# Two chained cross-attentions on one core: the last four heads' image outputs moved to GpSimd, the image softmax's shift moved within its step, and unread products in eleven steps

## The chip, the core and the metric

The kernel runs on one core of a Trainium2 chip. The metric is device time in microseconds (us) of one execution. Five engines work side by side, each through its own instructions in order: PE multiplies matrices (its weight loads are listed apart, as PEld), DVE (VectorE), ACT (ScalarE) and POOL (GpSimd) work element by element, and SP here only issues transfers (DMAs). [...]

## The reference

The input is x, 64 batches of 256 tokens with 320 channels, and a context of 77 rows of 512 per batch, of which the last four are image rows. Two layers follow each other; both have 20 heads of 16 channels and end with a projection, a bias and the residual. Layer 0 attends to the context. Layer 1 is this, for one batch:

```python
text_ehs, ip_ehs = encoder[:, :-4], encoder[:, -4:]
probs_t = softmax(q @ k_t * scale)               # 73 text rows
text_out = probs_t @ v_t
qsem = l2norm(probs_t @ text_ehs)
sem = qsem @ l2norm(ip_ehs)                       # 4 image rows
probs_ip = softmax(q @ k_ip * scale + 0.5 * sem) * spatial_mask
ip_out = probs_ip @ v_ip
out = (text_out + ip_out) @ W_out + b_out + residual
```

(The program's layer 0 takes all 77 rows in one softmax as its text, since layer 0's text length is 77 and leaves no image rows.) All of it is computed in float32.

## The kernel before

**Pairs, units, steps.** The batches go in 32 pairs p. A pair holds 1024 channel-major values of x per channel block: two blocks of 128 channels ("main") and a third of 64 for each batch, both batches stacked on 128 partitions ("last"). A unit is one batch, 128 tokens and eight heads; `UNITS` lists five of them per batch, the fifth being the last four heads (16 to 19) of both token halves. So a pair has ten units, and the main loop over g has ten steps for each pair. In the text, p and k are g divided by ten, and the remainder; a turn is the ten steps of one p. Step g works on layer 0's unit g and on layer 1's unit g - 13 (`LAG`), so layer 1 of a pair is one to two turns behind layer 0.

**One step.** In PSUM a single tile sc (L1082, one buffer) takes three results in turn: `semantics` (L755 and L761: layer 1's exponentials of the step before against the Gram matrix of the context, the values and ones), then `scores` (L641) of both layers. DVE takes each layer's row maximum (mx, L659) and subtracts it (w, L661); ACT exponentiates (L669, L672 and L673); for layer 0 DVE sums (L687, L688) and GpSimd normalizes (`normalize`, L692). PE transposes the exponentials of the unit before (L705, L706; layer 1's first, then layer 0's), ACT copies them out (L712, L713, L731, L732), and `attend` (L788, L793) multiplies layer 0's by the values. DVE multiplies the semantics by the weights (prod, L772 and L775) and ACT copies the text sums out of sc (sums, L1064); only then may the next step's L755 write sc. Each step ends with L1136.

**Fillers.** `fillers(k, p)` lists other work by step in three lists that the loop puts at three places: projections of queries, keys, values and outputs (L334, L379, L528 to L570, L616), the Gram matrix (`gram`, L493: PE, then two ACT copies, three small GpSimd operations and nine DMAs), the masked keys (`keys_by_head`, L365, GpSimd), the placing of values and Gram matrix into the matrices gv and gr that `semantics` multiplies by (`place_values`, L424 to L444, and `place_gram`, L511 and L515, GpSimd). A helper, `keep_order` (L46), ties the instructions of PE, ACT, DVE and GpSimd to the order in which the loop writes them; only SP's order of transfers is left to the scheduler after the first turn. The last steps, which have few fillers, hold unread transposes of the identity (`keep_busy`, L741).

**Layer 1's image part.** When the fifth unit of a batch has its semantics (k=9 for the pair's first batch, k=4 for the second), GpSimd squares the text's sums (least, L866), DVE completes the norms (L870, L882), `text_output` (an, L821 and L850) divides the text outputs by their sums, token by token. One step later `image_scores` (L883, L884) forms the four image scores of each head (num), two steps later `image_shifted` (L889 on DVE, L890 on GpSimd) subtracts their maximum and `image_exponential` (L893, ACT) follows, at the start of the step; three steps later `image_weights` (L900 to L902, L850) normalizes them into iw. `text_transposed` (L837, L838) turns an into aT at k=0 and k=5, in three transposes for each 128 tokens: two for main and one for last. At k=7 PE transposes the weights of all 20 heads (`image_transposed`, L914). The image values are in DRAM rows (vip_rows): for each batch, twenty DMAs (L475) put copies of its four rows under each other, and a GpSimd multiplication by ip_mask (L480) keeps of copy h the channels of head h only. `image_attend` (L926) multiplies these for main at k=8, ACT copies the result (L936) and GpSimd adds it to main (L938); `image_attend_last` (L947) does it for last, in two matmuls over 80 rows, and DVE adds (L951). Then `project` (L528, L537) runs at k=9 and `project_last` (L616) at the next k=0.

Of the kernel before, what the change touches and what calls it, by code (L numbers as in the profile page):

```python
# [14 lines left out]
H = 20  # L15
D = 16
# [47 lines left out]
def tile_two_cross_attentions(ctx: ExitStack, tc: tile.TileContext, a: dict, out: bass.AP):  # L64
# [179 lines left out]
    head_mask = blocks("head_mask", P, 8, D)  # L244
    for n in (4, 2):
        nc.gpsimd.tensor_add(head_mask[:, :n], head_mask[:, :n], head_mask[:, n : 2 * n])
    ip_mask = blocks("ip_mask", H * NIP, H, NIP)

# [218 lines left out]

    def image_values(p, b):  # L470

        n, r0 = H * NIP, (2 * p + b) * NIP
        vip = vips[p, b] = big.tile([n, C], F32, tag="vip", name=f"vip{p}_{b}", bufs=3)
        for h in range(H):
            nc.sync.dma_start(vip[h * NIP : (h + 1) * NIP, :], vip_rows[r0 : r0 + NIP, :])  # L475

    def place_image_values(p, b):
        n, vip = H * NIP, vips[p, b]
        v = vip.rearrange("p (h d) -> p h d", d=D)
        nc.gpsimd.tensor_tensor(v, v, ip_mask[:n].unsqueeze(2).broadcast_to([n, H, D]), ALU.mult)  # L480

    grams = {}

# [247 lines left out]
        nc.scalar.copy(pt[:, :, s * P : (s + 1) * P], ps)  # L731
        nc.scalar.copy(rt[:, s * P : (s + 1) * P], pr[:n, 0, :])  # L732

    def keep_busy(n):


        if n:
            ps = ptr.tile([P, 4, P], F32, tag="tr", name=f"busy{len(busy)}")
            busy.append(n)
            for i in range(n):  # L740
                nc.tensor.transpose(ps[:, i % 4, :], ident, ident)  # L741
# [72 lines left out]
            nc.scalar.copy(last, ps[:, 1, :])  # L814


    def text_output(p, b):

        sums = stats[p, b][1]
        rec = small.tile([P, 2 * H], F32, tag="rec", name=f"rec{p}_{b}", bufs=2)  # L820
        nc.vector.reciprocal(rec, sums[:, :, NIP + D])  # L821
        an = big.tile([P, 2, H, D], F32, tag="an", name=f"an{p}_{b}", bufs=1)
        by_head(an, sums[:, :, NIP : NIP + D], rec)
        return an

    def text_transposed(p, b):

        an = made["an"]
        if b == 0:
            aTs[1, p] = channels("aT1", f"aT1_{p}", 1)  # L830
        main, last = aTs[1, p]
        rows = slice(b * HALF, (b + 1) * HALF)
        for s in range(2):
            ps = ptr.tile([P, 4, P], F32, tag="tr", name=f"atr{p}_{b}{s}")
            t = an[:, s].rearrange("p h d -> p (h d)")
            for i in range(2):
                nc.tensor.transpose(ps[:, i, :], t[:, i * P : (i + 1) * P], ident)  # L837
            nc.tensor.transpose(ps[: rows.stop, 2, :], t[:, C - rows.stop :], ident)  # L838
            t0 = b * S + s * P
            nc.scalar.copy(main[:, :, t0 : t0 + P], ps[:, :2])  # L840
            nc.scalar.copy(last[rows, s * P : (s + 1) * P], ps[rows, 2, :])

    one = const.tile([P, 1], F32, tag="one", name="one")

    def by_head(to, t, factor):

        n = t.shape[2]
        for s, h0, at in ((0, 0, 0), (1, HT, H), (1, 0, H + 4)):
            m = H if s == 0 else H - HT if h0 else HT
            nc.gpsimd.tensor_tensor(  # L850
                to[:, s, h0 : h0 + m], t[:, at : at + m],
                factor[:, at : at + m].unsqueeze(2).broadcast_to([P, m, n]), ALU.mult,
            )


    nums = {}
# [38 lines left out]
    def image_weights(p, b):  # L895

        num = nums[p, b]
        m = small.tile([P, 2, H], F32, tag="imx", name=f"imx{p}_{b}", bufs=1)
        r = m.rearrange("p s h -> p (s h)")
        nc.vector.tensor_reduce(r, num, AX.X, ALU.add)  # L900
        nc.vector.reciprocal(r, r)
        nc.gpsimd.tensor_mul(m, m, smask.unsqueeze(2).broadcast_to([P, 2, H]))  # L902
        to = weights[p, b] = small.tile([P, 2, H, NIP], F32, tag="iw", name=f"iw{p}_{b}", bufs=2)
        by_head(to, num, r)

    weights = {}

    def image_transposed(p):
        n = H * NIP
        ps = ptr.tile([P, 4, P], F32, tag="tr", name=f"itr{p}")  # L910
        for b in range(2):
            w = weights[p, b].rearrange("p s h t -> p s (h t)")
            for s in range(2):
                nc.tensor.transpose(ps[:n, 2 * b + s, :], w[:, s], ident)  # L914
        wT = big.tile([n, S2], F32, tag="iwT", name=f"iwT{p}", bufs=1)
        nc.scalar.copy(wT, ps[:n].rearrange("p j t -> p (j t)"))
        return wT
# [22 lines left out]
        t = big.tile([P, 2, S2], F32, tag="ip_out", name=f"ip_out{p}", bufs=1)  # L940
        return [lambda i=i: out_of(i) for i in range(2)]

    def image_attend_last(p):
        wT, last = made["wT"], aTs[1, p][1]
        ps = pms.tile([P, 512], F32, tag="ms", name=f"ipv{p}_2")
        for b in range(2):
            nc.tensor.matmul(  # L947
                ps[b * HALF : (b + 1) * HALF, :S], vips[p, b][:, 2 * P :], wT[:, b * S : (b + 1) * S],
                start=True, stop=True,
            )  # L950
        nc.vector.tensor_add(last, ps[:, :S], last)  # L951


    made = {}

    def fillers(k, p):
# [19 lines left out]
        elif k == 1:  # L976
# [3 lines left out]
                add(1, p, place_values, 0, p, 0)  # L980
            add(0, p, queries, 0, p, 2)
            add(1, p - 1, project, 0, p - 1)
            add(1, p - 1, place_gram, 0)
            add(1, p, keys_by_head, 0, p, 1)
            add(1, p - 1, keys_by_head, 1, p - 1, 0)
# [9 lines left out]
        elif k == 3:  # L995
            add(0, p + 1, load_context, p + 1)
            add(0, p - 1, queries, 1, p - 1, 2)
            if p == 0:
                add(1, p, image_keys, 0)
            add(1, p - 1, queries, 1, p - 1, 1)  # L1000
            add(1, p, place_values, 0, p, 1)
            add(1, p - 1, keys_by_head, 1, p - 1, 1)
        elif k == 4:
            if p == 0:
                add(0, p, image_keys, 1)
            else:
                add(0, p, keys, 1, p, 0)
            add(1, p - 1, values, 1, p - 1, 1)
            add(1, p + 1, first_queries, p + 1)
        elif k == 5:  # L1010
            if p == 0:
                add(0, p, image_keys, 2)
            add(0, p + 1, keys, 0, p + 1, 0)
            add(2, p - 2, text_transposed, p - 2, 1)
        elif k == 6:
            while len(made_rows) * P < min(NB, 2 * (p + 2)) * T:
                rows_todo.extend((len(made_rows), l) for l in range(2))
                made_rows.append(rows_todo[-1])
            for n in range(len(rows_todo) // 2):
                add(0, p, value_rows, *rows_todo.pop(0))  # L1020
            if p == 0:
                add(0, p, image_norms)
            else:
                add(1, p, keys, 1, p, 1)
            add(1, p - 1, gram, p - 1, 1)
            add(1, p, place_image_keys, p)
        elif k == 7:
            add(0, p + 1, keys, 0, p + 1, 1)
            add(1, p + 1, last_keys, p + 1)
            add(1, p - 2, lambda: made.update(wT=image_transposed(p - 2)))  # L1030
            add(1, p - 1, place_values, 1, p - 1, 1)
            add(1, p - 1, image_values, p - 1, 0)
            if p == 0:
                add(1, p, image_rows)
        elif k == 8:
            while rows_todo:
                add(0, p, value_rows, *rows_todo.pop(0))
            add(1, p - 1, place_gram, 1)
            add(1, p + 1, keys_by_head, 0, p + 1, 0)
            add(1, p - 1, image_values, p - 1, 1)  # L1040
            add(1, p - 2, image_attend_last, p - 2)
            add(3, p - 2, lambda: held.update(i=lambda: image_attend(p - 2)))
        else:
            add(0, p - 2, project, 1, p - 2)
            add(1, p + 1, values, 0, p + 1, 0)
            for b in range(2):
                add(1, p - 1, place_image_values, p - 1, b)
# [18 lines left out]
            image_least(*before1[:2])  # L1066

    last0 = last1 = before1 = None
    later, early = {}, {}
    for g in range(NP * NU + LAG + 12):  # L1070
        p, k = divmod(g, NU)
        first, second, third, begin = fillers(k, p)
# [25 lines left out]
        for l in range(2):  # L1098
            if now[l]:
                shifted(ps, l, *now[l])  # L1100
        new1 = None
        if last1:
            transposed(1, *last1)
# [23 lines left out]
            sums_out(ps)  # L1127
        if now[1]:
            exponential(1, g, *now[1])
        for fn, args in later.pop(g, ()):  # L1130
            fn(*args)
        if now[0]:
            normalize(g)
        if before1:
            q, b, u = before1[:3]
            nc.vector.tensor_reduce(eight(stats[q, b][2], u), prod, AX.X, ALU.add)  # L1136
            if ends:
                image_squares(q, b)
                made["an"] = text_output(q, b)
                later[g + 1] = [(image_scores, (q, b))]  # L1140
                early[g + 2] = [(image_shifted, (q, b)), (image_exponential, (q, b))]
                early[g + 3] = [(image_weights, (q, b))]
        for fn, args in second:
            fn(*args)
# [3 lines left out]
                attend(q, b, int(u > 1))  # L1148
        for fn, args in third:
            fn(*args)  # L1150
        if ends:
            image_norm(*before1[:2])
        last0 = (*now[0], ws[0]) if now[0] else None
# [53 lines left out]
```

## Time and profile before

| | us |
|---|---|
| median of 3 runs | 2615.54 (2613.35 to 2617.14) |
| the profiled execution | 2612.19 |
| its span, first to last instruction | 2610.4 |
| busy: PE | 2552.0 (98%) |
| busy: DVE | 1971.3 (76%) |
| busy: ACT | 1535.6 (59%) |
| busy: POOL | 1439.9 (55%) |
| DMA packets of the main queue | 153432, 18.0% of 16 engines |
| granted PE clock, mean | 0.998 |

A row of the profile reads: start or line, engine, operation, the written tile and the read ones (`out<-in`), shapes as partitions x elements, and how many. In brackets stands the idle time before it and what ended it. A matmul's own duration is longer than its share of PE's time, since the next one starts before it ends; for PE it is the distance of starts that counts.

### The profile page before, as it was taken

The page shows a single profiled execution, that of the slowest core. Times are in us where ns is not written, and L with a number is a line of the kernel's source. Part 1 is how long each engine was busy: PE and PEld are TensorE (multiplying, and loading weights), DVE is VectorE, ACT ScalarE, POOL GpSimd, SP SyncE. Part 2 cuts the span into 40 slices and gives each one's busy share as a digit, 9 for nine tenths or more (in the row PEclk, how much of TensorE's full clock was granted, in tenths as well). Part 3 has the DMA queues.
Part 4 walks back from the last instruction along what each step waited for, and adds up shares of the span by engine and source line. Part 5 has one row for each costly group of instructions (what it writes and reads, how often), then busy time and mean ns, then how long its engine had stood idle before and what let it go on. Part 6 is the DMA issues. An engine that isn't in the chain of part 4 may idle for free.

```text
span 2610.4 us, 74097 instructions
## 1 busy us (share of the span) xinstructions
PE 2552.0 (98%) x27026; PEld 1979.1 (76%) x27026; DVE 1971.3 (76%) x3641; ACT 1535.6 (59%) x3989; POOL 1439.9 (55%) x3514
## 2 busy tenths in 40 slices
PE   7999999999999999999999999999999999999998
PEld 5677777777777777777777777777777777777677
DVE  4577777777787777787777787777777778777864
ACT  3465665665665665665665665665665566666553
POOL 2456555566555556555556555556555565555542
PEclk9999999999999999999999999999999999999999
DMA  5212211112111112111112111112111112111100
GB/s 164 72 29 58 58 43 48 43 51 55 52 51 38 51 51 55 55 48 39 51 52 55 51 52 43 47 52 56 52 51 39 51 53 55 47 50 34 29 22 23
DMA packets 154658, 132.28 MB, mean 51 GB/s; under 512 B 48248, under 2 KB 132984, under 8 KB 154296
## 3 DMA queue, kind: packets, MB, share of 16 engines
q1 hardware_dynamic: 153432, 126.38, 18.0%
q8 instruction: 217, 3.56, 0.6%
q14 instruction: 145, 1.19, 0.2%
q10 hardware_dynamic: 864, 1.15, 0.1%
HBM read 89.53 MB, written 33.91 MB: 47 GB/s over the span
## 4 chain that ended last, share of the span: by engine, by line
PE 84%; DVE 7%; DMA 3%; ACT 2%; POOL 1%; issue 1%; SPq 1%; DVEq 0%; POOLq 0%; ACTq 0%
PE sc L755 12%; PE tr L705 11%; PE o_ps L528 8%; PE sc L641 7%; PE v_ps L379 6%; PE sc L761 4%; PE q_ps L528 4%; PE q_ps L555 4%; PE k_ps L334 3%; PE o_ps L616 3%; DVE w L661 3%; PE pv L788 2%; PE o_ps L537 2%; DVE mx L659 2%; PE q_ps L557 2%; PE rtr L706 2%
## 5 line engine op out<-in xcount | busy, mean ns | idle before, releaser
L659 DVE TENSOR_REDUCE mx<-sc 128x8 f32<-128x584 f32 (+1 forms) x640 | 497.3, 777 | 446.9 <-PE sc L641 446.8
L692 POOL TENSOR_TENSOR parts<-w,sm 128x512 f32<-128x512 f32 (+1 forms) x640 | 439.5, 707 | 301.9 <-ACT parts L673 177.8
L661 DVE TENSOR_TENSOR w<-sc,mx 128x616 f32<-128x616 f32 x640 | 511.8, 800 | 67.0 <-ACT w L669 0.5
L712 ACT COPY pt<-tr 128x512 f32<-128x512 f32 x320 | 186.8, 584 | 431.9 <-PE tr L705 427.5
L705 PE MATMUL tr<-ident,parts 128*128 128x128 f32 x2560 | 409.6, 283 | 12.5 <-POOL parts L692 5.2
L755 PEld LDWEIGHTS sc<-gv,pt 64*128 64x128 f32 x5120 | 316.9, 187 | 96.0 <-ACT sums L1064 47.3
L705 PEld LDWEIGHTS tr<-ident,parts 128*128 128x128 f32 x2560 | 282.5, 141 | 123.4 <-issue 88.0
L755 PE MATMUL sc<-gv,pt 64*128 64x94 f32 x5120 | 356.3, 278 | 17.4 <-ACT sums L1064 17.2
L676 POOL COPY att<-w 128x32 f32<-128x32 f32 x320 | 66.8, 209 | 469.7 <-DVE w L661 469.2
L669 ACT ACTIVATE w<-w 128x616 f32<-128x616 f32 x320 | 232.0, 725 | 96.7 <-DVE w L661 95.8
L687 DVE TENSOR_REDUCE sm<-w 128x8 f32<-128x616 f32 x320 | 247.9, 775 | 13.6 <-ACT w L669 13.6
L641 PE MATMUL sc<-kbd,q 32*128 32x154 f32 x5120 | 248.2, 306 | 1.0 <-ACT q L586 0.8
L528 PE MATMUL o_ps<-aT,wo 128*128 128x256 f32 x1024 | 231.6, 379 | 0.0
L1136 DVE TENSOR_REDUCE nrm<-prod 128x8 f32<-128x584 f32 x320 | 227.3, 710 | 0.4
L772 DVE TENSOR_TENSOR prod<-sc,parts 128x512 f32<-128x512 f32 x320 | 217.8, 681 | 4.0 <-PE sc L761 4.0
L528 PEld LDWEIGHTS o_ps<-aT,wo 128*128 128x128 f32 x1024 | 189.7, 190 | 23.0
L672 ACT ACTIVATE parts<-w 128x512 f32<-128x512 f32 x320 | 207.1, 647 | 0.0
L641 PEld LDWEIGHTS sc<-kbd,q 32*128 32x128 f32 x5120 | 187.0, 187 | 6.2 <-issue 5.4
L731 ACT COPY pt<-tr 128x512 f32<-128x512 f32 x256 | 151.1, 590 | 67.1 <-PE tr L705 66.8
L379 PE MATMUL v_ps<-wv,cf 128*128 128x320 f32 (+1 forms) x624 | 182.1, 438 | 0.0
L706 PE MATMUL rtr<-ident,parts 128*104 128x128 f32 (+1 forms) x640 | 174.8, 273 | 0.0
L1064 ACT COPY sums<-sc 128x168 f32<-128x168 f32 x320 | 96.4, 301 | 122.5 <-DVE prod L775 121.3
(151 smaller groups left out, 4840.0 us busy)
## 6 DMA issues: line engine op xcount, KB each, us to landing
vip<-vip_rows SPq DMA_DIRECT2D x1280, 5.0 KB
out_dram<-x SPq DMA_DIRECT2D x64, 256.0 KB
x<-in_x_dram SPq DMA_DIRECT2D x31, 512.0 KB
v_rows<-vs SPq DMA_DIRECT2D x38, 320.0 KB
vm<-v_rows SPq DMA_DIRECT2D x152, 80.0 KB
ct<-in_ctx_dram SPq DMA_DIRECT2D x32, 308.0 KB
cf<-in_ctx_dram SPq DMA_DIRECT2D x38, 256.0 KB
g_rest<-gram_rest SPq DMA_DIRECT2D x512, 0.5 KB
```

The costliest lines, as they stand in the source:

```text
L379: nc.tensor.matmul(ps[:n, :C], cfs[i][:, k, :n], wv[l][:, k, :], start=(k == 0), stop=(k == KE - 1))
L528: nc.tensor.matmul(ps[b][:, m, :], w[:, k, m * P : (m + 1) * P], main[:, k, b * S : (b + 1) * S], start=(k == 0 and m == 0), stop=False,)
L641: nc.tensor.matmul(ps[:, r, 2 * T * l : 2 * T * (l + 1)], q[rows, b, :] if part == 2 else q[rows, t0 : t0 + P], kbd[rows, part].rearrange( ...
L659: nc.vector.tensor_reduce(mx, sc[:, :, :, :nt], AX.X, ALU.max)
L661: nc.vector.tensor_tensor(w, sc, mx.unsqueeze(3).broadcast_to([P, 4, 2, T]), ALU.subtract)
L669: nc.scalar.activation(w, w, AF.Exp, scale=SCALE)
L687: nc.vector.tensor_reduce(sm, w, AX.X, ALU.add)
L692: nc.gpsimd.tensor_tensor(two[:, 8 * t0 : 8 * t1].rearrange("p (h t) -> p h t", h=8), w[:, :, t0:t1], sm.unsqueeze(2).broadcast_to([P, 8, ...
L705: nc.tensor.transpose(ps[:, i, :], flat[:, i * P : (i + 1) * P], ident)
L706: nc.tensor.transpose(pr[:n, 0, :], flat[:, 4 * P : 4 * P + n], ident)
L755: nc.tensor.matmul(ps[:, i % 2 * 2 + j, at : at + GV], pt[half_rows, i, :], gv[b][half_rows, part, i, :], start=start and i < 2, stop=False,)
L1136: nc.vector.tensor_reduce(eight(stats[q, b][2], u), prod, AX.X, ALU.add)
```

## The change

Four things change.

1. The last four heads' image outputs. Each batch's image values are loaded for 16 heads (sixteen DMAs of 256 channels), the weights are transposed for 16 heads, and `image_attend_last` is gone. In its place a DMA spreads the batch's four rows of the last 64 channels over all 128 partitions (vlast, one buffer), and GpSimd multiplies them, token by token, by the weights of the last four heads and adds the products to the text output (four times a multiplication and an addition, each 128 wide). The last heads' text outputs of both batches go into one tile (an_last); `text_transposed` transposes main alone, and two transposes and one copy (`last_transposed`, at k=8) bring an_last into last. `last_image_outputs` runs at k=4 for the first batch and at k=7 for the second.
2. The shift. `image_shifted` stands behind both layers' subtractions, before layer 1's transposes, in place of the start of the step; `image_exponential` goes into the list `later`, and that list is put behind `normalize` in place of before it. So `image_scores` stands behind `normalize` too.
3. Two fillers move: the second batch's `gram` from k=6 to k=5, and its `place_values` from k=7 to the end of GpSimd's work of k=8.
4. `keep_busy` can use the PSUM pool of the fillers (ms), and eight unread transposes are put at the end of the steps g = 6, 7, 9, 10, 18, 19 and of 314 to 318 (p=31, k=4 to 8).

```diff
     def image_values(p, b):
-        n, r0 = H * NIP, (2 * p + b) * NIP
-        vip = vips[p, b] = big.tile([n, C], F32, tag="vip", name=f"vip{p}_{b}", bufs=3)
-        for h in range(H):
-            nc.sync.dma_start(vip[h * NIP : (h + 1) * NIP, :], vip_rows[r0 : r0 + NIP, :])
+        n, r0 = HT * NIP, (2 * p + b) * NIP
+        vip = vips[p, b] = big.tile([n, 2 * P], F32, tag="vip", name=f"vip{p}_{b}", bufs=3)
+        for h in range(HT):
+            nc.sync.dma_start(vip[h * NIP : (h + 1) * NIP, :], vip_rows[r0 : r0 + NIP, : 2 * P])
...
+    def last_image_values(p, b):
+        r0 = (2 * p + b) * NIP
+        v = vips[p, b, "last"] = small.tile([P, NIP, HALF], F32, tag="vlast", name=f"vlast{p}_{b}", bufs=1)
+        nc.sync.dma_start(v, vip_rows[r0 : r0 + NIP, 2 * P :].unsqueeze(0).broadcast_to([P, NIP, HALF]))
...
-            nc.tensor.transpose(ps[: rows.stop, 2, :], t[:, C - rows.stop :], ident)
             t0 = b * S + s * P
             nc.scalar.copy(main[:, :, t0 : t0 + P], ps[:, :2])
-            nc.scalar.copy(last[rows, s * P : (s + 1) * P], ps[rows, 2, :])
+    def last_image_outputs(p, b):
+        v = vips[p, b, "last"].rearrange("p t (h d) -> p t h d", d=D)
+        w, to = weights[p, b, "last"], lasts[p][:, :, b]
+        part = [P, 2, H - HT, D]
+        for t in range(NIP):
+            prod = small.tile(part, F32, tag="ip_last", name=f"ip_last{p}_{b}{t}", bufs=1)
+            nc.gpsimd.tensor_tensor(
+                prod, v[:, t].unsqueeze(1).broadcast_to(part), w[:, :, :, t].unsqueeze(3).broadcast_to(part), ALU.mult
+            )
+            nc.gpsimd.tensor_add(to, to, prod)
+    def last_transposed(p):
+        ps = pms.tile([P, 512], F32, tag="ms", name=f"ltr{p}")
+        for s in range(2):
+            nc.tensor.transpose(
+                ps[:, s * P : (s + 1) * P], lasts[p][:, s].rearrange("p b h d -> p (b h d)"), ident
+            )
+        nc.scalar.copy(aTs[1, p][1], ps[:, :S])
...
-    def image_attend_last(p):
-        wT, last = made["wT"], aTs[1, p][1]
-        ps = pms.tile([P, 512], F32, tag="ms", name=f"ipv{p}_2")
-        for b in range(2):
-            nc.tensor.matmul(
-                ps[b * HALF : (b + 1) * HALF, :S], vips[p, b][:, 2 * P :], wT[:, b * S : (b + 1) * S],
-                start=True, stop=True,
-            )
-        nc.vector.tensor_add(last, ps[:, :S], last)
...
+            add(1, p - 2, last_image_values, p - 2, 0)
...
+            add(1, p - 2, last_image_outputs, p - 2, 0)
...
+            add(1, p - 1, gram, p - 1, 1)
             add(2, p - 2, text_transposed, p - 2, 1)
+            add(1, p - 2, last_image_values, p - 2, 1)
...
-            add(1, p - 1, gram, p - 1, 1)
...
-            add(1, p - 1, place_values, 1, p - 1, 1)
+            add(1, p - 2, last_image_outputs, p - 2, 1)
...
-            add(1, p - 2, image_attend_last, p - 2)
+            add(1, p - 1, place_values, 1, p - 1, 1)
+            add(1, p - 2, last_transposed, p - 2)
...
+        if g in middle:
+            fn, args = middle.pop(g)
+            fn(*args)
         new1 = None
         if last1:
             transposed(1, *last1)
...
+        if now[0]:
+            normalize(g)
         for fn, args in later.pop(g, ()):
             fn(*args)
-        if now[0]:
-            normalize(g)
...
-                early[g + 2] = [(image_shifted, (q, b)), (image_exponential, (q, b))]
+                middle[g + 2] = (image_shifted, (q, b))
+                later[g + 2] = [(image_exponential, (q, b))]
                 early[g + 3] = [(image_weights, (q, b))]
...
+        if g in (6, 7, 9, 10, 18, 19) or -6 <= idle <= -2:
+            keep_busy(8, pms, "ms")
```

## The prediction

> **What bounds the kernel now.** I read the busy times on the profile's page first, then the waits, then the timeline of one steady turn (the ten steps of one p; here p=15, from 1167 us on), then the last 30 us.
>
> ```profile
> span 2610.4 us, 74097 instructions
> ...
> PE 2552.0 (98%) x27026; PEld 1979.1 (76%) x27026; DVE 1971.3 (76%) x3641; ACT 1535.6 (59%) x3989; POOL 1439.9 (55%) x3514
> ...
> PE 84%; DVE 7%; DMA 3%; ACT 2%; POOL 1%; issue 1%; SPq 1%; DVEq 0%; POOLq 0%; ACTq 0%
> ```
>
> PE is nearly always busy and carries the chain, so what counts is PE's own work per step, until a step gets so short that the next shortest chain ends it. A step begins at its first L755 row. Read off these rows, the median steps k=0 to 9 last 8.08, 9.39, 8.61, 7.45, 8.69, 6.42, 6.95, 6.96, 7.09 and 7.81 us, and hardly vary from turn to turn. The boundary k=5 to k=6, PE's rows:
>
> ```profile
> 1215.26 0.38 PE L837 MATMUL atr<-ident,an 128*128 128x128 f32 x2
> 1215.47 0.27 PE L838 MATMUL atr<-ident,an 128*128 128x128 f32 x1
> 1216.07 1.13 PE L755 MATMUL sc<-gv,pt 64*128 64x94 f32 x16 [0.32 <-ACT sums L1064]
> ```
>
> Here PE is out of work: only one buffer holds sc, and L755 may not write it before DVE has done mx, w, mx, w, prod and ACT the copy sums. That chain (mx starts 2.06 to 2.16 us into a step, sums ends 6.36 to 6.54) is the floor of a step: 6.42 in k=5, 6.59 in steps 314 and 318. Nine of ten steps stand above it and are PE's.
>
> **The edits, step by step.** (Pitch means from one start to the next; a transpose's is 0.11 us, as in L837's two rows.)
>
> *k=0 and k=5, text_transposed.* Each loses two third transposes (L838): 0.22 us. In k=0 that is gained. In k=5 the moved gram comes in: its eight L493 rows hold PE from 1222.39 to 1223.02, 0.63 us, and cost 0.53 here, since what follows L706 then starts 0.11 after it instead of 0.20. PE's work was 6.42 - 0.39 = 6.03 and becomes 6.03 - 0.22 + 0.53 = 6.34, under the floor: k=5 stays at 6.42, and gram is free there.
>
> *k=6.* Without gram PE has 6.95 - 0.63 and, for the changed neighbour of L755, + 0.08 = 6.40. But the shift's DVE reduction L889 (309 ns) now stands between the second w and prod. Followers start about 0.08 before the end of the one ahead, so it adds 0.23 to the floor: sums ends at 6.44 in this step (1222.51), L755 follows 0.05 after it, 6.44 + 0.05 + 0.23 = 6.72. Gain 0.23. In the six turns with two value rows in k=6 (9.10 us) PE still binds and the gain is 0.55.
>
> *k=8.*
>
> ```profile
> 1236.28 0.27 PE L706 MATMUL rtr<-ident,parts 128*104 128x128 f32 x1
> 1236.37 0.30 ACT L1064 COPY sums<-sc 128x168 f32<-128x168 f32 x1
> 1236.48 0.20 PEld L947 LDWEIGHTS ipv<-iwT,vip 80*64 80x64 f32 x4 [0.18 <-issue]
> 1236.49 0.65 PE L947 MATMUL ipv<-iwT,vip 80*64 80x256 f32 x4
> ```
>
> From L706 to the next L755 (1237.07) are 0.79 us. Two transposes in L947's place make 0.11 + 0.11 + 0.20 = 0.42. Sums ends at 6.69 in this step, so the floor is 6.74: 7.09 becomes 6.74, a gain of 0.35. The new transposes wait for GpSimd's second sums, ready at 5.65 by the paragraph after the next; PE comes to them at 6.39, so 0.7 covers them, and behind them only L755 waits. The transposes of the weights lose columns (80 to 64) and nothing in time: L706's 104 and 128 columns both pass in 0.11.
>
> *k=1.* ACT's exponential L893 stood ahead of the copies pt and pr and waited for GpSimd until 3.35 us into the step; the second transposes, which need those copies' PSUM buffers, began at 4.31. In k=3, the same work without it, they begin at 4.17. L893 goes behind the exponentials: 0.14 gained. Its reader in k=2 (L900) sits in DVE's wait for PE.
>
> *GpSimd.* The other splits come out even: an's three products took 744 + 295 + 631 and become 631 + 400 + 631, the mask L480 shrinks from 728 to about 630. Per pair 16 operations of 128 wide are new. Multiplications: 295 ns at 64 and 631 at 256 (L850); L464, 128 wide, took 400, which I take. Additions: 523 at 160 (L884), so 0.45. Each waits for the one before, and L883 to L884 shows 0.07 between such. Eight take 4 x 0.85 + 7 x 0.07 = 3.9 us (bounds 2.8, all at the 64-wide row, and 5.5, all at the 256-wide one). The first eight run in k=4 and 5, where GpSimd was idle from 1211.3 to 1215.0. The second eight take the place of place_values, which goes from k=7 to behind the masked keys in k=8, into this gap:
>
> ```profile
> 1240.85 0.44 POOL L365 TENSOR_TENSOR kbd<-kl,head_mask 128x154 f32<-128x154 f32 x1
> 1244.82 0.27 POOL L866 TENSOR_TENSOR least<-sums 128x40 f32<-128x40 f32 x1 [3.52 <-ACT sums L1064]
> ```
>
> From k=8's start: normalization ends at 1.73, the eight at 5.65; then by their rows' pitches L938 2.31, att 0.17, L692 1.32, L511 0.92, L515 0.27, L365 1.06, place_values 3.48: 15.2. Steps 8 and 9 now last 14.55, so it ends 0.6 into k=0. Its last product is read by L761, 1.06 into k=0: 0.4 us to spare. Behind it least comes 0.65 later, and DVE's L870 and the four x of k=0 with it; g_ps needs the third x, at 1.83 + 0.65 = 2.48, and starts at 2.62: covered.
>
> *SP and DMA.* Per pair 40 small loads become 32 and two broadcasts. The broadcast into the single vlast buffer makes SP wait for GpSimd: in k=5, where SP stood idle anyway (the waits give SP 341.0 us for PE's g_ps), and in k=8 until 5.7. Behind that one are the second image values, read 10 us later in k=0, then the next text values, read in k=1. Broadcasts are 32,768 packets of 256 B; at the mean of the profile's page (18.0% of 16 engines over 153,432 packets, 49 ns) the share goes from 18 to 22%. I cost both at nothing; bound 0.3 us a turn if SP's delay reached GpSimd.
>
> *Eleven fillers* of eight transposes, 0.9 us each. Steps 18, 19 and 314 end at the floor with PE idle over 0.9: free. So are 6, 9 and 10, since each next transpose waits for parts. Step 7 is dense: +0.9. 315 and 317 end on PE: +0.9 each; 316 gets the 0.23, 318 0.2: +2.2. What they could win is the clock:
>
> ```profile
> 75.10:78.50 3.40, 1.78 (x21) 1.38 (x21) 2.48 (x5) 1.47 (x4) 2.43 (x4) 1.00 0.54 146
> 78.50:85.50 7.00, 5.87 (x59) 3.30 (x56) 2.57 (x5) 2.15 (x7) 4.00 (x8) 0.51 0.32 83
> 143.40:146.80 3.40, 1.34 (x26) 1.28 (x28) 3.21 (x7) 2.46 (x7) 1.16 (x3) 1.00 0.59 182
> 146.80:150.30 3.50, 3.50 (x38) 3.19 (x35) 2.75 (x5) 3.30 (x7) 3.38 (x7) 0.51 0.02 4
> 2584.50:2593.00 8.50, 7.92 (x72) 7.32 (x69) 3.55 (x9) 4.79 (x10) 3.59 (x8) 1.00 0.00 0
> ```
>
> (Busy time of PE, PEld, DVE, ACT, POOL, then granted clock.) After stretches with PE 52 and 39% busy the clock fell to half, which cost about 1.5 us in step 10 (the pv rows last 3.64 instead of step 20's 1.95) and 1.4 in step 20. I count half: -1.5. The last row is nothing but transposes, at full clock.
>
> [...]
>
> *Tail.* After pair 31's last text_output GpSimd now runs eight operations before num (1.58 us of an from 2587.08, then 2589.48 becomes 2592.6), +3.1. The second eight follow iw for 3.9; from iw's end (2593.81) to the end of the main sums (L934, 2597.73) are 3.9 too, so both reach the projection together. PE then idles 3 us before itr; a half clock after it would cost up to 3.5, I take 1.5. The other late steps give back 0.5.
>
> **Sum.** Turn: -0.22 - 0.14 - 0.23 - 0.35 = -0.94; 29 turns (pairs 2 to 30) -27.3; six longer k=6, -1.9; step 16, -0.35; last turn -0.36 + 2.2; start +0.9 - 1.5; tail +3.1 + 1.5 - 0.5. Total -24.2. The profiled execution took 2612.2 us (span 2610.4); the median 2615.5 is 3.3 higher, and I subtract from it: **2591**. A measurement of this kernel tells about 0.2% (5 us) from no change.
>
> **Rivals.**
> A (slower): GpSimd overruns in k=8 and 9. If the eight take over 4.3 us, L761 waits in every turn, and each 0.1 us costs 2.9. Break-even is 5.1 us (24.2 / 29 = 0.83 over). At the bound of 5.5 the wait is 1.2 x 29 = 35: 2591 + 35 = 2626. For it: only 0.4 to spare, and no row of this exact form. Against: L464 and L884. 0.15.
> B: the floor takes the gains of k=6 and k=8 (a slower sums or L889): 0.58 x 29 = 17 less, 2608. For: both new lengths lie on the floor, not on PE. Against: the floor was 6.36 to 6.69 in all rows. 0.13.
> C: the change does not do what it says: the fillers leave the clock as it was, 2591 + 1.5, about 2593. 0.10.
> Forecast 0.57; 0.05 for better than 2583 (chance stalls in k=4, up to 1.2 us, going as well).
> The range 2583 to 2613 leaves out that 0.05 and nearly all of A. Faster: 0.57 + 0.10 + 0.05 + 0.08 of B = 0.80; same: 0.05 of B, 0.03 of A; slower 0.12.
>
> **What would show it.** Steps of 7.86, 9.25, 6.42, 6.72 and 6.74 us in k=0, 1, 5, 6, 8, with L755 released by sums after the last three; a row of 128 wide additions near 450 ns; the least row within 0.9 us of k=0's start; full clock at 78 and 147 us; num 3 us later at the end. L761 or PE's transposes waiting for GpSimd would prove me wrong.

## Result, and the profile after

| | before | after |
|---|---|---|
| median, us | 2614.53 (2613.35 to 2617.14, 4 runs) | 2591.53 (2590.22 to 2594.47, 4 runs) |
| the profiled execution (span), us | 2612.19 (2610.4) | 2590.22 (2588.5) |

The ratio is 0.9912, 95% interval 0.9895 to 0.9929: the change makes the kernel about 23 us faster. The head of the page after, and its chain by engine:

```profile
span 2588.5 us, 74021 instructions
...
PE 2536.5 (98%) x26922; PEld 1977.1 (76%) x26922; DVE 1958.5 (76%) x3609; ACT 1520.3 (59%) x3893; POOL 1653.5 (64%) x4026
...
PE 89%; DVE 5%; ACT 2%; DMA 1%; POOL 1%; issue 1%; SPq 1%; DVEq 0%; ACTq 0%; POOLq 0%
```

GpSimd works 214 us more and PE is still the bound. The lengths of the steps, read off the first semantics rows as before (medians of steps 20 to 309; the sums are over these 29 turns; L755 is now L762; k=3 and k=9 kept their lengths, 0.00 and +0.07 us in all):

| k | before | forecast | after | sum forecast | sum measured |
|---|---|---|---|---|---|
| 0 | 8.08 | 7.86 | 8.02 | -6.4 | -3.15 |
| 1 | 9.39 | 9.25 | 9.29 | -4.1 | -3.81 |
| 2 | 8.61 | 8.61 | 8.51 | 0 | -3.17 |
| 4 | 8.69 | 8.69 | 8.69 | 0 | -1.67 |
| 5 | 6.42 | 6.42 | 6.42 | 0 | +0.09 |
| 6 | 6.95 | 6.72 | 6.82 | -8.6 | -6.53 |
| 7 | 6.96 | 6.96 | 6.88 | 0 | -2.17 |
| 8 | 7.09 | 6.74 | 6.75 | -10.2 | -9.77 |
| all ten | | | | -29.2 | -30.10 |

Outside the turns: the first twenty steps +0.1 and the start ahead of them +0.4, steps 310 to 313 -0.3, 314 to 318 +2.9, 319 to 333 -0.4, from step 334 to the end +5.4. In all -22.0, as the two spans say (2610.4 to 2588.5).

The boundary k=6 to k=7 after (compare the one shown of before, k=5 to k=6):

```profile
1206.66 0.80 DVE L668 TENSOR_TENSOR w<-sc,mx 128x616 f32<-128x616 f32 x1
...
1207.38 0.31 DVE L921 TENSOR_REDUCE most<-num 128x40 f32<-128x160 f32 x1
...
1207.60 0.68 DVE L779 TENSOR_TENSOR prod<-sc,parts 128x512 f32<-128x512 f32 x1
...
1208.46 0.30 ACT L1093 COPY sums<-sc 128x168 f32<-128x168 f32 x1 [0.30 <-DVE prod L782]
...
1208.81 0.46 PE L762 MATMUL sc<-gv,pt 64*128 64x94 f32 x4 [0.33 <-ACT sums L1093]
```

The shift's reduction stands between w and prod, prod comes 0.22 later for it, and PE now waits 0.33 us for sums: k=6 has gone onto the floor. The end of k=8:

```profile
1221.76 0.43 ACT L380 COPY vs<-v_ps 128x320 f32<-128x320 f32 x1 [0.75 <-PE v_ps L379]
...
1222.08 0.30 ACT L1093 COPY sums<-sc 128x168 f32<-128x168 f32 x1
1222.10 0.38 PE L867 MATMUL ltr<-ident,an_last 128*128 128x128 f32 x2
...
1222.43 0.58 PE L762 MATMUL sc<-gv,pt 64*128 64x94 f32 x6
```

Two transposes stand where two matmuls stood, and L762 follows sums by 0.05 us. The start of k=0 (it begins at 1230.25):

```profile
1230.96 0.27 POOL L898 TENSOR_TENSOR least<-sums 128x40 f32<-128x40 f32 x1
...
1231.27 0.20 DVE L902 SCALAR_TENSOR_TENSOR nrm<-least,nrm 128x40 f32<-128x40 f32 x1 [1.06 <-POOL least L898]
...
1231.70 1.56 DVE L608 SCALAR_TENSOR_TENSOR x<-o_ps,bo,x 128x256 f32<-128x256 f32 x4
...
1232.92 0.76 PE L500 MATMUL g_ps<-ct 128*73 128x77 f32 x8
```

The same rows of the kernel before, where this step begins at 1244.88:

```profile
1245.55 1.56 DVE L601 SCALAR_TENSOR_TENSOR x<-o_ps,bo,x 128x256 f32<-128x256 f32 x4
...
1247.51 0.70 PE L493 MATMUL g_ps<-ct 128*73 128x77 f32 x8
```

In the changed kernel DVE waits 1.06 us for least, so the four x end at 3.01 instead of 2.22 us into the step, and g_ps starts at 2.67 instead of 2.62. PE's rows behind it are 0.09 to 0.17 us later than before. The end:

```profile
2561.24 0.41 POOL L858 TENSOR_TENSOR ip_last<-vlast,iw_last 128x128 f32<-128x128 f32 x1
2561.72 0.46 POOL L861 TENSOR_TENSOR an_last<-an_last,ip_last 128x128 f32<-128x128 f32 x1
...
2565.22 0.49 POOL L915 TENSOR_TENSOR num<-sums,nrm 128x160 f32<-128x160 f32 x1
```

The eight operations take 3.98 us ahead of num. And the clock, in five stretches (busy time of PE, PEld, DVE, ACT, POOL, then granted clock):

```profile
75.40:78.80 3.40, 1.91 (x19) 1.29 (x18) 2.46 (x4) 1.77 (x4) 1.42 (x3) 1.00 0.44 121
144.10:147.50 3.40, 1.83 (x31) 1.53 (x33) 2.97 (x7) 2.46 (x6) 2.96 (x14) 1.00 0.18 49
147.50:151.00 3.50, 3.50 (x33) 3.19 (x29) 2.79 (x6) 3.46 (x8) 3.50 (x7) 0.51 0.10 19
2567.60:2571.00 3.40, 1.71 (x12) 1.35 (x14) 0.72 (x2) 0.58 (x1) 2.25 (x7) 1.00 0.00 0
2571.00:2577.80 6.80, 6.80 (x27) 5.72 (x26) 1.29 (x2) 0.37 (x1) 2.19 (x5) 0.50 0.00 0
```

The half clock at 78 us is gone (1.00 from 78.8 to 85.8 us), the one in step 20 has stayed (0.51), and the end has a new one of 6.8 us (0.50).

### The profile page after: what moved, and what is told of

It reads as the page before. It is cut to its first block, busy times and chain, and to the rows that moved or that the text cites. A ratio compares the mean times of both kernels' runs of the same rounds, so it can differ in the third digit from the quotient of the medians.

```text
span 2588.5 us, 74021 instructions
## 1 busy us (share of the span) xinstructions
PE 2536.5 (98%) x26922; PEld 1977.1 (76%) x26922; DVE 1958.5 (76%) x3609; ACT 1520.3 (59%) x3893; POOL 1653.5 (64%) x4026
## 3 DMA queue, kind: packets, MB, share of 16 engines
q1 hardware_dynamic: 185176, 132.41, 18.6%
## 4 chain that ended last, share of the span: by engine, by line
PE 89%; DVE 5%; ACT 2%; DMA 1%; POOL 1%; issue 1%; SPq 1%; DVEq 0%; ACTq 0%; POOLq 0%
PE sc L762 13%; PE tr L712 12%; PE o_ps L535 8%; PE sc L648 7%; PE sc L768 5%; PE v_ps L379 4%; PE q_ps L562 4%; PE q_ps L535 4%; PE k_ps L334 4%; PE o_ps L623 4%; PE pv L795 3%; PE o_ps L544 3%; PE pv L800 3%; PE q_ps L570 2%; PE rtr L713 2%; PE q_ps L564 2%
## 5 line engine op out<-in xcount | busy, mean ns | idle before, releaser
L762 PEld LDWEIGHTS sc<-gv,pt 64*128 64x128 f32 x5120 | 316.8, 187 | 88.2 <-ACT sums L1093 44.2
L762 PE MATMUL sc<-gv,pt 64*128 64x94 f32 x5120 | 356.3, 278 | 12.8 <-ACT sums L1093 10.4
```

The lines of the kernel that those rows point to most:

```text
L762: nc.tensor.matmul(ps[:, i % 2 * 2 + j, at : at + GV], pt[half_rows, i, :], gv[b][half_rows, part, i, :], start=start and i < 2, stop=False,)
```

## Experiments

All kernels but the third and fourth are made from the changed one; lines are its own unless said. The kernel before was timed again beside each (2614.5 to 2616.1 us). Medians of neighbouring kernels often lie within each other's intervals; the lengths of the steps repeat from trace to trace to a few hundredths of a microsecond and tell more.

**1. No fillers.**

```diff
-        if g in (6, 7, 9, 10, 18, 19) or -6 <= idle <= -2:
-            keep_busy(8, pms, "ms")
```

> The changed kernel without its eleven fillers of eight unread transposes; all else stays. Theory (the fillers in dense steps cost PE their own length, and hold the clock once): steps 314 to 318 get 2.5 us shorter together, steps 5 to 9 2.0 us shorter, and the half clock at 78 us comes back, which puts 1.7 us into steps 10 and 11; the whole is 2 to 3 us less than the changed kernel, 2589. Rival (the clock is held by something else in the change): no half clock at 78 us, 4.5 us less, 2587. Second rival (the fillers hold more of the clock than the trace shows): a half clock in the last steps as well, 2593 or more.

Measured 2590.16 us (ratio 0.9902, 0.9887 to 0.9917): not told apart from the changed kernel. Steps 5 to 9 lost 1.6 us and no half clock came at 78, as the first rival had it; but two of 6.8 us came in the last turn, at 315 and 318 (step 319 is 2.9 longer), as the second had it. The theory's time came out and its reason did not.

**2. The second batch's shift at the start of the step.**

```diff
+        for fn, args in ahead.pop(g, ()):
+            fn(*args)
         if now[0]:
             normalize(g)
...
-                later[g + 1] = [(image_scores, (q, b))]
-                middle[g + 2] = (image_shifted, (q, b))
+                (ahead if b else later)[g + 1] = [(image_scores, (q, b))]
+                if b:
+                    early[g + 2] = [(image_shifted, (q, b))]
+                else:
+                    middle[g + 2] = (image_shifted, (q, b))
```

> The changed kernel, but for the second batch of each pair the image scores stand ahead of the normalization and the shift at the start of the step again, as in the kernel before; its exponential stays behind the normalization, and the first batch keeps the new order. Theory (the shift's reduction between the second w and prod is all that k=6 waits for): sums ends 0.33 us earlier in k=6, which falls from 6.82 to 6.49 in the 23 turns without value rows there, 7.6 us in all, 2584. The prediction's own term (0.23 us a turn) gives 2586. Rival (PE's own work of k=6, 6.40 by the prediction's sum, is really as long as the step): k=6 stays at 6.82 or falls by less than 0.1 us, 2590 to 2591.5.

Measured 2587.60 (0.9892, 0.9876 to 0.9907). k=6 is 6.49, to the hundredth. The same boundary in this kernel, where L762 starts 6.49 into the step and 0.05 behind sums:

```profile
1204.36 0.80 DVE L668 TENSOR_TENSOR w<-sc,mx 128x616 f32<-128x616 f32 x1
...
1205.08 0.68 DVE L779 TENSOR_TENSOR prod<-sc,parts 128x512 f32<-128x512 f32 x1
...
1205.93 0.30 ACT L1093 COPY sums<-sc 128x168 f32<-128x168 f32 x1
...
1206.28 0.35 PE L762 MATMUL sc<-gv,pt 64*128 64x94 f32 x2
```

k=6 gave 7.3 us, but k=7 went from 6.88 back to 6.95 in every turn (+2.4 with one stall): part of what the shift's new place costs in k=6 it gains in k=7 (experiment 10 says how). One stall of 4.1 us in step 254 and a half clock in step 317 (1.6 us) took more.

**3. The last heads' outputs as before** (from the kernel before, with the second, third and fourth part alone).

> The kernel before with the second, third and fourth part of the change alone: the last heads' image outputs stay on PE and DVE. Theory, by the steps that the two traces show: k=8 is longer than in the changed kernel by 0.34 us, k=0 by 0.05, k=5 by 0.14 (PE's work there is 6.56 with the third transposes and the Gram matrix, 0.14 over the floor), 0.53 x 29 = 15.4 us, and the end is 4.5 us shorter: 11 us more than the changed kernel, 2602.5. Rival (the first part pays only for its own tail, and the gain is the other parts'): within 2 us of the changed kernel.

Measured 2619.38 (1.0016, 1.0006 to 1.0026): 17 us over the theory, and slower than the kernel before. k=8, k=0 and k=5 came as the theory says (7.09, 8.08, 6.56). What it did not have are stalls in k=4, 16.2 us in all, of 4 to 5 us in steps 64, 204 and 254, each followed by a half clock, and two more half clocks in the last turn. Step 254 of this kernel begins at 1985.55:

```profile
1992.17 0.72 POOL L453 TENSOR_TENSOR v<-vm,half 128x320 f32<-128x320 f32 x1 [5.38 <-DMA v_rest<-v_rows]
...
1994.45 0.44 POOL L365 TENSOR_TENSOR kbd<-kl,head_mask 128x154 f32<-128x154 f32 x1
1994.52 0.28 ACT L337 COPY kT<-k_ps 128x146 f32<-128x146 f32 x1 [4.30 <-POOL kbd L365]
...
1994.86 2.59 PE L528 MATMUL q_ps<-x,wq 128*128 128x256 f32 x7 [3.25 <-ACT kT L337]
```

Read it upwards: PE waits for ACT's copy, which waits for GpSimd's masked keys, which stand behind layer 0's place_values (the one that was moved is layer 1's, in k=8), which waits for a transfer in SP's queue.

**4. The same with place_values in k=7 again.**

```diff
         elif k == 7:
+            add(1, p - 1, place_values, 1, p - 1, 1)
...
         elif k == 8:
-            add(1, p - 1, place_values, 1, p - 1, 1)
```

> The kernel before with the second and fourth part of the change and the Gram matrix in k=5, but place_values again in k=7 (the third experiment's kernel without that move). There k=4 held stalls of 16.2 us in all (4.1 to 5.2 us in three turns with value rows) and half clocks behind them. Theory (place_values in k=8 frees the text values' buffer later, SP waits there, and with 40 small image loads a pair the next values come late in the turns with value rows): the stalls fall to the 3 us of the kernel before, the half clocks go with them, about 18 us less than the 2619.4 of that kernel, 2600 to 2603. Rival (the stalls come from the moved Gram matrix's transfers, or from chance): 2612 to 2620.

Measured 2606.70 (0.9964, 0.9951 to 0.9976). The stalls of k=4 fall to 3.1 us and the half clocks behind them go; L453 of step 254 (which begins at 1975.92) starts 2.0 us earlier in its step:

```profile
1980.53 0.72 POOL L453 TENSOR_TENSOR v<-vm,half 128x320 f32<-128x320 f32 x1 [3.37 <-DMA v_rest<-v_rows]
```

So the moved place_values made them. In the changed kernel it stands in k=8 too, and yet L453 starts 4.0 us into step 254 and k=4 holds 0.9 us of stalls: there SP has 34 image loads a pair in place of 40, in another order. Which of the two spares it was not tried. The kernel also gives the second part and gram without the first: k=1, 2, 6 and 7 are as in the changed kernel, k=5 is 6.56. It is 15 us slower than the changed kernel: that much the first part is worth, together with the place that it makes for place_values in k=8, its longer end included.

**5. One more GpSimd multiplication in k=8.**

```diff
             nc.gpsimd.tensor_add(to, to, prod)
+        if b:
+            nc.gpsimd.tensor_tensor(
+                prod, v[:, 0].unsqueeze(1).broadcast_to(part), w[:, :, :, 0].unsqueeze(3).broadcast_to(part), ALU.mult
+            )
```

> The changed kernel with one more GpSimd multiplication of 128 elements (0.41 us and a gap of 0.07, its result is not used) behind the second batch's eight operations, so that place_values and least come 0.49 us later into k=0. Theory (k=0 already waits for least through L902, x and g_ps, so nothing is to spare): every turn gets 0.45 to 0.49 us longer in k=0, 13 to 14 us in all, 2605. Rival (the prediction's reading: the first reader is L768 at 1.06 us, 0.4 us later than place_values ends, and g_ps is covered): 0.09 us a turn, 2.6 us, 2594.

Measured 2602.70 (0.9948, 0.9935 to 0.9962). k=0 went from 8.02 to 8.47, 0.45 us for 0.49, in 21 turns and by 0.44 in step 110, and not at all in the six turns behind a k=8 with value rows. That makes 9.9 us; step 20, where the half clock of the changed kernel did not come, is 0.5 shorter. The two profiled executions are 12.9 us apart: a half clock in step 325 brought 1.7, one in step 6 1.7 too, of which step 7 gave 0.9 back, k=4 0.9 and step 310 0.5. The wait is in the row of g_ps of this kernel:

```profile
1237.98 0.76 PE L500 MATMUL g_ps<-ct 128*73 128x77 f32 x8 [0.35 <-DVE x L608]
```

Nothing was to spare: the theory, and not the reading of the prediction.

**6. The square root's input behind the four x.**

```diff
-                image_squares(q, b)
+                if b:
+                    image_squares(q, b)
+                else:
+                    after_drains[g + 1] = (q, b)
...
         for fn in drains:
             fn()
+        if g in after_drains:
+            image_squares(*after_drains[g])
+            image_norm(*after_drains.pop(g))
```

> The changed kernel, but for the first batch the square root's input (L902 on DVE, which waits for GpSimd's least) and its square root stand behind the projection's four outputs x of k=0 instead of ahead of them. Theory (in k=0 PE's g_ps waits for the third x, which waits for L902, which waits for GpSimd's place_values): x starts at 0.2 instead of 1.45 us into the step, g_ps no longer waits, and k=0 falls from 8.02 to 7.85 us, 0.17 x 29 = 4.9 us, 2586.5. Rival (PE's own order sets k=0, and the eight shorter steps are short for another reason): k=0 stays at 8.02, 2591.5; or the later square root holds ACT's copies and k=0 gets longer, 2592 to 2597.

Measured 2589.51 (0.9902, 0.9887 to 0.9917). k=0 fell to 7.87 in the 21 turns that had 8.02, 3.3 us in all; step 20 is 0.5 shorter for want of its half clock, and step 90 0.25 longer. A half clock in step 6 (1.7 us, of which step 7 gave 0.3 back) and k=4 (0.8) hide a part of it in the profiled run. In this kernel step 160 begins at 1229.83 and the four x start at 0.21:

```profile
1230.04 1.56 DVE L608 SCALAR_TENSOR_TENSOR x<-o_ps,bo,x 128x256 f32<-128x256 f32 x4
...
1231.52 0.48 DVE L902 SCALAR_TENSOR_TENSOR nrm<-least,nrm 128x40 f32<-128x40 f32 x1
...
1232.46 0.70 PE L500 MATMUL g_ps<-ct 128*73 128x77 f32 x8
```

**7. The last pair's end.** (For the last pair, last_transposed also takes its PSUM tile from the pool of the other transposes, ptr.)

```diff
         elif k == 3:
...
+            if p == NP + 1:
+                add(1, p - 2, last_image_outputs, p - 2, 0)
         elif k == 4:
...
-            add(1, p - 2, last_image_outputs, p - 2, 0)
+            if p < NP + 1:
+                add(1, p - 2, last_image_outputs, p - 2, 0)
...
         elif k == 8:
...
-            add(1, p - 2, last_transposed, p - 2)
+            if p < NP + 1:
+                add(1, p - 2, last_transposed, p - 2)
         else:
             add(0, p - 2, project, 1, p - 2)
+            if p == NP + 1:
+                add(1, p - 2, last_transposed, p - 2)
```

> The changed kernel with two changes for the last pair alone: the first batch's eight operations run one step earlier, where GpSimd has nothing to do, so that they no longer stand ahead of num; and last_transposed stands behind the projection's first sixteen matmuls instead of ahead of them. Theory (the end is a chain through GpSimd's eight operations, num, iw, the eight of the second batch and the transposes): num comes 4.0 us earlier, the projection starts when the main sums are there, 1 to 2 us earlier still; from step 334 to the end 27 to 28 us instead of 32.8, 2586. Rival (what the end costs is the half clock between 2571 and 2578 us, which PE's idle time brings either way): the end gets 2 to 4 us shorter, 2588 to 2589.5, with the half clock still there.

Measured 2585.08 (0.9883, 0.9868 to 0.9897). From step 334 to the end 27.30 us: all of the 5.4 came back, and the half clock is gone as well. The same stretches of this kernel as above:

```profile
2567.60:2571.00 3.40, 3.40 (x25) 2.59 (x23) 1.29 (x2) 0.09 (x1) 2.62 (x7) 1.00 0.00 0
2571.00:2577.80 6.80, 4.98 (x29) 3.83 (x30) 1.42 (x4) 0.37 (x1) 0.00 (x0) 1.00 0.00 0
```

**8. The three together** (2, 6 and 7).

> The changed kernel with three experiments together: the second batch's shift at the start of the step, the square root's input behind the four x of k=0, and the two changes of the last pair. Theory (the three act in different places and add up, as steps): k=6 6.49 and k=7 6.95 (4.9 us less in all), k=0 7.87 (4.4 us less), the end 5 us shorter: 2577. Rival (the gains of k=6 and k=0 are given back as stalls in k=4 or as half clocks, as both experiments' medians suggest, 3.9 us instead of 4.9 and 2.0 instead of 3.5): 2581 to 2584.

Measured 2577.39 (0.9854, 0.9838 to 0.9871): they add up as steps (k=0 7.86, k=6 6.49, k=7 6.95, the end 27.2).

**9. The Gram matrix in k=6 again** (gram's line moved back).

> The changed kernel with the second batch's Gram matrix in k=6 again. Theory (in k=5 it stood in PE's idle time under the floor, and in k=6 the floor of 6.82 now hides most of it): k=5 stays at 6.42, k=6 goes from 6.82 to 6.95, which PE's work of 6.40 and the matrix's 0.55 make, and the six turns with value rows get 0.53 longer: 23 x 0.13 + 6 x 0.53 = 6 us, 2597.5. Rival (the matrix costs its 0.55 us wherever it stands, since PE's work and the chain through DVE add up): k=5 falls to 5.9 or k=6 rises to 7.35, the one 15 us faster and the other 15 us slower with it.

Measured 2601.29 (0.9949, 0.9936 to 0.9961). k=5 stays at 6.42 and k=6 is 6.95; steps 20 to 309 are 6.1 us longer, the 6 of the theory. The other 4 are probably half clocks: in this profile one of 6.8 and one of 10.2 us stand in the last turn, which is 6.6 us longer; what stood in the other runs was not recorded.

**10. A wait taken off the subtraction** (on the kernel of the three).

```diff
+        if k in (6, 7, 8) and now[0] and g - 2 in parts_of:
+            nc.vector.tensor_copy(small.tile([P, 1], F32, tag="seen", name=f"seen{g}", bufs=1), parts_of[g - 2][:, 8 * M : 8 * M + 1])
...
+        if now[0]:
+            parts_of[g] = ws[0]
```

> The kernel with the three experiments together, and in k=6, 7 and 8 one more DVE instruction ahead of mx, where DVE is idle: it copies one element of the normalized parts of two steps before, so that DVE's next subtraction w has no wait for GpSimd of its own. Theory (w starts 0.10 us after mx where it waits for GpSimd too, and 0.03 where it doesn't, though GpSimd's instruction had ended long before): k=6 from 6.49 to 6.42, k=7 from 6.95 to 6.88 through the copy pt, k=8 from 6.75 to 6.72, where PE's own work is next; 1.6 + 2.0 + 0.7 = 4.3 us less than that kernel's 2577.4, 2573. Rival (the 0.07 us come from GpSimd working at the same time, not from the wait): all three stay, 2577 to 2578.

Measured 2576.76 (0.9851, 0.9837 to 0.9864). The first w in k=7 of the kernel of the three, and then with the added copy:

```profile
1207.10 0.80 DVE L666 TENSOR_REDUCE mx<-sc 128x8 f32<-128x616 f32 x1 [0.32 <-PE sc L648]
1208.01 0.80 DVE L668 TENSOR_TENSOR w<-sc,mx 128x616 f32<-128x616 f32 x1
```

```profile
1205.87 0.80 DVE L666 TENSOR_REDUCE mx<-sc 128x8 f32<-128x616 f32 x1 [0.30 <-PE sc L648]
...
1206.71 0.80 DVE L668 TENSOR_TENSOR w<-sc,mx 128x616 f32<-128x616 f32 x1
```

0.91 from start to start became 0.84, while GpSimd's rows at that time are the same, and k=7 fell to 6.88. What goes is an instruction: where w waits for GpSimd too, the trace has a semaphore instruction of DVE between mx and w (517 at this line in the kernel of the three, 451 with the added copies). k=6 did not move, since there the early shift had already done the waiting. Nor did k=8: its sums start at the same place, behind ACT's copy vs, which waits for PE's v_ps (the k=8 lines of the changed kernel show the same order). So two of the three places were wrong and the mechanism right, worth 1.7 us; the median can't tell that.

**11 and 12. The same without fillers, and with the late ones alone.**

> The kernel of the waits' experiment without all eleven fillers. Theory (a half clock comes where a stretch of 3.4 us has PE busy for half of it or less, which here depends on chance, and the fillers do not settle it): the fillers' own 2.0 us in steps 5 to 9 and 2.5 in 314 to 318 go, and half clocks come back in some runs for 0 to 3 us: 2572 to 2576, against 2576.8 with them. Rival (the fillers hold the clock): half clocks in steps 10, 20 and 314 to 318 in the profiled run, 2577 to 2581.

> The same with the five late fillers alone. Theory: steps 5 to 9 get 2.0 us shorter, and one half clock at most is left before step 21, as in the runs with the early fillers: 2574 to 2576. Rival (the early fillers hold the clock): half clocks in steps 10 and 20 both, 1.4 to 1.7 us each, 2577 to 2579.

Measured 2573.96 (0.9842, 0.9829 to 0.9856) and 2574.69 (0.9850, 0.9836 to 0.9863), both within their theory's range and 2 to 3 us below the kernel with all eleven, but not told apart from it by their intervals. The profiled run without fillers was its slowest, 2581.8: half clocks in steps 6 and 20, and in the last turn for 6.8 and 20.5 us:

```profile
2420.00:2423.40 3.40, 1.14 (x14) 0.89 (x12) 3.27 (x6) 2.23 (x7) 0.71 (x4) 1.00 0.13 33
2423.60:2430.40 6.80, 6.24 (x54) 5.39 (x52) 5.18 (x10) 4.88 (x10) 5.93 (x13) 0.50 0.00 1
```

Over the fourteen profiles: a half clock in the last turn in 4 of 11 with the late fillers and 2 of 3 without; before step 21, 7 in ten profiles with the early ones and 6 in four without. That leans to the fillers as a cover for the bad runs, and not to a gain at the median.

## Why the prediction came out, step by step

The time was right to 0.5 us (2591 for 2591.53), and the turn to 1 us in 30. Several terms inside were not, and cancelled. The hit at 2591 is in part luck: the sum starts from a median of 2615.5 of the kernel before, which measured 2614.5 beside the result, and the change itself was -23.0 us between the medians and -22.0 between the traces, where -24.2 was summed.

*k=8 and k=5* held. k=8 fell by 0.34 of the forecast 0.35, and k=5 stayed on its floor with gram in it; experiment 9 shows that its 0.55 us are free there. But what k=8 stands on is not the chain through DVE that the prediction calls the floor: sums follows ACT's copy vs, which waits for PE's v_ps, and when experiment 10 moved w and prod 0.07 us forward, sums stayed where it was.

*k=6*: the mechanism was right, the size not. The floor rose by 0.33 and not 0.23; the missing 0.10 lies in the two subtractions (the second begins 4.67 us into the step, before at 4.57), since L921 no longer stands ahead of them. Experiment 2 shows that nothing else holds k=6.

*k=2 and k=7*, 5.3 us that the prediction did not have, are the other side of this. In the trace before, the first w of k=2 and k=7 waits for GpSimd as well as for mx; in the changed kernel the late L921 of k=1 and k=6 has waited for GpSimd ahead of it, the trace has no such wait at this w, and w starts 0.03 behind mx in place of 0.10. In k=7 this reaches PE through ACT's copies (itr starts at 5.32 for 5.39), in k=2 through DVE's x and L564. Experiments 2 and 10 show it for k=7 by taking it away and putting it back; for k=2 it is read from the traces alone.

*k=1* gave 0.10 of the 0.14 through the moved exponential; the second transposes start at 4.17 as forecast, but the projection behind them gains only 0.11 (4.77 for 4.88).

*k=0* is the step that failed: "g_ps needs the third x, at 1.83 + 0.65 = 2.48, and starts at 2.62: covered". least came 0.78 later and not 0.65, the third x ended at 2.61, g_ps waited, and of 0.22 us three quarters went. Experiments 5 and 6 show the chain from both sides. With it falls the 0.4 us to spare of rival A: its slope begins at once, 9.9 us for 0.49 over 22 turns.

*GpSimd's new operations* were well priced: 0.41 and 0.457 us, 4.03 for eight, where 3.9 was taken. A's overrun did not come; but a smaller one was there all the time, through x and not through L768.

*SP and DMA at nothing*: k=4 even gained 1.7 us of stalls. The risk was larger than the bound of 0.3 us a turn, as experiment 3 shows with a neighbouring order of the same edits. The share of the main queue of 16 engines rose from 18.0 to 18.6% and not to 22: the 32,768 new packets of 256 B took 17 ns each and not the mean packet's 49, and the image loads got shorter.

*The clock*: the half clock of step 10 went and that of step 20 stayed, which is the half that was counted, but not for the fillers' sake: it was absent without them too (experiments 1, 11 and 12). So rival C holds in the sense that the fillers' worth can't be shown. The fillers themselves cost more than counted: 1.66 in step 315 for 0.9, and 0.87, 0.59 and 0.65 in steps 6, 9 and 10, which were held to be free. The two falls were mis-sized as well: step 10 lasted 7.23 us with its half clock and lasts 5.19 with neither that nor a filler (experiments 1, 11 and 12), 2.0 and not 1.5; step 20 lasted 8.09 and is 7.58 in experiment 3, where the clock stayed full, 0.5 and not 1.4. *The end* cost 5.4 where 4.6 were summed (3.1 + 1.5): the eight operations took 4.0 ahead of num. That the half clock is the rest is not shown, since experiment 7 takes both away.

*B* was a size and not a case: the floor took 0.10 in k=6 and, whatever sets it, nothing in k=8.

## What to carry to other kernels

When an engine gets work, follow its next result to the last engine that waits for it, not to its first reader: here the first reader had 0.4 us to spare, and a second, through another engine's queue, had none. When a step is on a floor, what counts is the order of that floor's own instructions, so put a small operation of a side chain where its engine waits anyway. At the two ends of a program, put the same work elsewhere than in the steady turns: 5.5 us, two thousandths of this kernel, lay in one pair's order.

## What the runs showed of the hardware

**Half clocks come on a grid, and PE's busy share did not settle where.** In the two traces of before and after they last 3.41 or 6.83 us, but for one at each program's end, and begin multiples of 3.413 us apart (78.54 and 146.81 us before, 20 of them; 147.56 and 2571.02 after, 710). The 10.2 and 20.4 us of experiments 9 and 11 are about three and six of them. On this grid PE was busy for 53 and 39% of the stretch ahead of the two half clocks before (from 75.13 and 143.39), and for 54 and 51% after (from 144.14 and 2567.61). Other stretches were not followed by one: 51, 53 and 45% before (from 2478.11, 2532.73 and 2604.41), 50, 56 and 48% after (from 55.40, 75.88 and 2564.20). So the half in the theory of experiment 11 is no line here. The same step falls in one run and not in the next: step 20 in the changed kernel, not in experiments 5 and 6. One fall of 3.41 us made step 20 0.5 us longer, and steps 6, 317 and 325 1.6 to 1.7; of step 6's, step 7 gave 0.3 to 1.1 back. In the four runs of experiment 12 the granted clock was 0.999 where they took 2573.1 to 2575.5 us, and 0.996 in the one of 2579.9.

**One more wait on w went with about 0.07 us of its start.** In the traces of before and after, a step's first w starts 0.10 us behind the end of mx where a semaphore instruction of DVE stands between the two (k=2, 3, 4, 7, 8 and 9 before; 1, 3, 4, 6, 8 and 9 after), and 0.03 where none does. In experiment 10, 0.91 from start to start became 0.84.
